# A time-mix layer with a GELU network beside it: k of the first block in halves of 256 tokens, and the third block's loads and statistics behind the first network

## The chip, the core and the metric

The kernel runs on one core of one Trainium2 chip. The metric is the time of one execution on the device in microseconds (us). Nine executions of the kernel before took 942.82 to 943.63 us, with a median of 943.16 us. The engines are called as the profile calls them: PE is TensorE (matmuls; PEld is its weight load), DVE is VectorE, ACT is ScalarE, POOL is GpSimd, and SP is SyncE, which issues nearly all DMAs here.

## The reference

The input x has 4 sequences of 1024 tokens with 512 channels, in float32. Cut to what matters:

```python
xn = (x - mean(x)) / sqrt(var(x) + 1e-5)                       # per token
# attention: a time mix with a decaying state
xx = concatenate([xn[:, 1:2], xn[:, :-1]], axis=1) - xn        # token before; token 1 for token 0
k = einsum('btc,hc->bth', xn + xx * mix_k, Wk)                 # 704 hidden channels
r = einsum('btc,hc->bth', xn + xx * mix_r, Wr)
w = exp(-exp(decay))
state[t] = state[t-1] * w + relu(k[t]);  y[t] = state[t] * r[t]
a = layernorm(einsum('bth,ch->btc', y, Wv)) * gamma + beta
# network on the same xn
d = gelu(float16(xn) @ W0.T + bias0).astype(float16)           # 2048 hidden channels
e = (d @ W1.T + bias1).astype(float16)
out = x + a + e
```

## The kernel before, in words

The tokens go through in 8 blocks of 512. Each block has an attention stage (k, r, the scan over time and the output product) and a network stage, and PE takes them in turn: attention of block 0, then the network of block 0, then attention of block 1, and so on. The 704 hidden channels are five full chunks of 128 (`full_chunks`, lines 391 to 403) and a half chunk of 64 (`half_chunk`, 408 to 421). A chunk's k is four matmuls of 128x512 in float32, one for each 128 channels of x, and so is its r; each float32 matmul shows as two records in the profile. After k, ACT applies the ReLU (line 374), DVE scans (376), and after r DVE multiplies (402). The output product is `attention_out` (425 to 475).

The network (`ffn`, 492 to 545) splits W0 and W1 into a high and a low fp32r part. For each of 16 chunks of its 2048 hidden channels, `up(n)` does eight matmuls into `pd`, ACT applies GELU (510), DVE casts (512), and `down` does eight matmuls into four accumulators `pe` (517). `up` runs two chunks ahead of `down`. In block 0 the network's weights are split while it runs: W0 at line 138, W1 at 153, each by an ACT cast to the high part and a DVE subtraction to the low part (124 and 125); the split W1 is also written to DRAM (154) and read from there by later blocks (156, 147).

For blocks 1 to 7 the inputs are made ahead, inside the network of the block before: `layernorm` (189) with statistics and normalisation on DVE and the inverse root on POOL, `transposed` (198) on DVE, and `mixed_inputs` (334). `load_x` (79) has one buffer, so x of block i+2 can be loaded as soon as block i+1 has been transposed. A scheduler orders the instructions of each engine by its own estimates of their readiness; it may put an instruction earlier than the program text has it.

Block 0 has no block before it, and `first_inputs` (209 to 332) makes its inputs. There the order on ACT, DVE and PE is written out by hand. Four tiles of 128 tokens each are normalised, transposed by PE into four PSUM banks `pts` (one for each 128 channels), and mixed: for each channel chunk and for k and r, ACT scales a copy (313) and DVE adds the token before, scaled (316). PE fills its waiting time with matmuls on the identity (`busy`, 228). Three small transposes belong to it: the mix vectors (282), the first two tokens (278), and the rows of decay and bias0 (295).

PSUM has four banks `ps_mm`, taken in rotation by all products but `pe`, and four banks `ps_e`. The queue of SP is issued in order, and a DMA issue can wait for an earlier DMA to land or for a buffer.

Of the kernel before, what the change touches and what calls it, by code (L numbers as in the profile page):

```python
# [19 lines left out]
def time_mix_and_gelu_ffn(  # L20
# [79 lines left out]
    rest_sb = const.tile([P, 2 * NC], F32, name="rest_sb")  # L100
    w_sb = const.tile([P, NF + 1], F32, name="w_sb")
    b0_sb = const.tile([P, NN], F32, name="b0_sb")
# [7 lines left out]
    nc.sync.dma_start(late_rows[:NF], rows(decay[:H0]))  # L110
    nc.sync.dma_start(late_rows[NF : NF + 1, :HF], decay[H0:].rearrange("(c p) -> c p", p=HF))
    nc.sync.dma_start(late_rows[NF + 1 :], rows(bias0))
    wk_sb = [const.tile([P, HID], F32, name=f"wk_{c}") for c in range(NC)]
    wr_sb = [const.tile([P, HID], F32, name=f"wr_{c}") for c in range(NC)]
    for c in range(NC):
        nc.sync.dma_start(wk_sb[c], wkT[c * P : (c + 1) * P, :])
        nc.sync.dma_start(wr_sb[c], wrT[c * P : (c + 1) * P, :])
    wv_sb = const.tile([P, NF + 1, C], F32, name="wv_sb")
# [21 lines left out]
    def load_w1(i, n):  # L140
        if i == len(blocks) - 1 and n == NN - 1:

            parts = [
                three.tile([P, C], F32R, tag="raw", name=f"w1_{i}_{n}_{p}") for p in range(2)
            ]
            for p in range(2):
                nc.sync.dma_start(parts[p].bitcast(F32), w1_dram[n][:, p, :].bitcast(F32))
            return parts
        w1 = wide.tile([P, 2, C], F32R, tag="w1", name=f"w1_{i}_{n}", bufs=3)
        if i == 0:  # L150
            raw = three.tile([P, C], F32, tag="raw", name=f"w1raw_{n}")
            nc.sync.dma_start(raw, w1T[n * P : (n + 1) * P, :])
            split(w1[:, 0, :], w1[:, 1, :], raw)
            nc.sync.dma_start(w1_dram[n].bitcast(F32), w1.bitcast(F32))
# [43 lines left out]
    def transposed(xn):  # L198
# [3 lines left out]
        for j in range(P // Q):  # L202
            for i in range(P // Q):
# [3 lines left out]
                )  # L207

    def first_inputs(xs, behind):


# [3 lines left out]
        idle = ps_mm.tile([P, TB], F32, tag="mm", name="idle")  # L215
        small = ps_mm.tile([P, TB], F32, tag="mm", name="small")
        tail = ps_mm.tile([P, TB], F32, tag="mm", name="tail")
        mix_t = small[:, : 2 * NC]
        late_t = tail[:, : NF + 1 + NN]
        edge = ps_mm.tile([P, TB], F32, tag="mm", name="edge")  # L220
        edge_t = edge[:, : NC * 2].rearrange("p (c t) -> p c t", t=2)
# [4 lines left out]
        xk = one.tile([P, NC, TB], F32, tag="xk", name="xk_0")  # L226

        def busy(n):
# [15 lines left out]
        def normalized(s):  # L244
            x_s, r = xs[:, s, :], rstd[:, s : s + 1]
            if s < 2:
                shift = shifts[:, s : s + 1]
                nc.vector.scalar_tensor_tensor(
                    shift, mv[:, s, 0:1], -1.0, r, ALU.mult, ALU.mult
                )  # L250
                nc.scalar.activation(x_s, x_s, AF.Identity, bias=shift, scale=r)
            else:
                normalize(x_s, x_s, mv[:, s, 0:1], r)

        def turned(s):
# [7 lines left out]
        steps = [(0, 0), (1, 0), (0, 1), (1, 1), (2, 0), (3, 0), (2, 1), (3, 1)]  # L263
        with tc.manual_schedule(
            engines={nc.scalar.engine, nc.vector.engine, nc.tensor.engine}
        ):

            nc.scalar.activation(shifts[:, :1], eps_sb, AF.Sqrt)
            busy(11)
            stats(0)  # L270
            stats(1)
            deviations(0)
            inverses(0)
            normalized(0)
            normalized(1)
# [6 lines left out]
            nc.tensor.transpose(mix_t, mix_rows, ident[: 2 * NC, : 2 * NC])  # L282
            busy(1)
            stats(2)
            stats(3)
            deviations(2)
            nc.scalar.copy(ends, edge_t)
            nc.scalar.copy(mix_sb, mix_t)
            nc.scalar.activation(rest_sb, mix_t, AF.Identity, bias=1.0, scale=-1.0)
            inverses(2)  # L290
            normalized(2)
            turned(2)
            normalized(3)
            turned(3)
            nc.tensor.transpose(
                late_t, late_rows, ident[: NF + 1 + NN, : NF + 1 + NN]
            )
            busy(5)
# [3 lines left out]
            for dst, m in ((xk[:, :, 0], mk_sb), (xnT[:, :, 1], mr_sb)):  # L302
                part = two.tile([P, NC], F32, tag="part", name="part")
                nc.vector.tensor_mul(part, apart, m)
                nc.vector.tensor_add(dst, part, ends[:, :, 0])
            for c, kind in steps:
                if kind == 0:
                    dst = part = xk[:, c, 1:]
                else:
                    ar = two.tile([P, TB], F32, tag="xx", name=f"ar_0_{c}")  # L310
                    dst, part = xnT[:, c, 2:], ar[:, 1:]
                j = kind * NC + c
                scaled = nc.scalar.activation(
                    part, pts[c][:, 1:], AF.Identity, scale=rest_sb[:, j : j + 1]
                )
                mixed = nc.vector.scalar_tensor_tensor(
                    dst, pts[c][:, : TB - 1], mix_sb[:, j : j + 1], part, ALU.mult, ALU.add
                )

        behind.enter_context(tc.issue_after(scaled.ins))  # L320
        behind.enter_context(tc.issue_after(mixed.ins))
        x16s = []
# [5 lines left out]

        nc.scalar.activation(w_sb, late_t[:, : NF + 1], AF.Exp)
        nc.scalar.activation(w_sb, w_sb, AF.Exp, scale=-1.0)  # L330
        nc.scalar.copy(b0_sb, late_t[:, NF + 1 :])
        return x16s, xk

# [31 lines left out]

    def attention(i, xk):

# [19 lines left out]

        def product(dst, w, cols, src, c):
            nc.tensor.matmul(dst, w[c][:, cols], src, start=(c == 0), stop=(c == NC - 1))  # L389

        def full_chunks():
            g = one.tile([P, NF, TB], F32, tag="g", name=f"g_{i}")
            for h in range(NF):
                cols = slice(h * P, (h + 1) * P)
                pk = ps_mm.tile([P, TB], F32, tag="mm", name=f"pk_{i}_{h}")
                for c in range(NC):
                    product(pk, wk_sb, cols, xk[:, c, :], c)
                st = states(h, P, pk)
                pr = ps_mm.tile([P, TB], F32, tag="mm", name=f"pr_{i}_{h}")
                for c in range(NC):  # L400
                    product(pr, wr_sb, cols, xnT[:, c, 1:], c)
                nc.vector.tensor_mul(g[:, h, :], st, pr)  # L402
            return g
# [79 lines left out]
    def finish(i, s, z, e16):  # L483
        b, t0 = blocks[i]

        width = C // 2 if i == len(blocks) - 1 and s == NS - 1 else C
        for c0 in range(0, C, width):
            cols = slice(c0, c0 + width)
            nc.vector.tensor_add(z[:, cols], z[:, cols], e16[:, cols])
            nc.sync.dma_start(out[b, t0 + s * P : t0 + (s + 1) * P, cols], z[:, cols])  # L490

    def ffn(i, xf, between, state):
# [52 lines left out]
        return pe  # L545

    behind = ExitStack()
    x16s, xk = first_inputs(x_now, behind)
    xf = ffn_input(0, x16s)

    state = {}
    full_chunks, half_chunk = attention(0, xk)
    g = full_chunks()
    gh = half_chunk()
    for i in range(len(blocks)):
# [6 lines left out]
        if more:  # L564
            x_now = load_x(i + 1)

# [3 lines left out]
        def next_norm():  # L570
            layernorm(i + 1, x_now)

# [3 lines left out]

        within = i == 0 or not more
        between = {0: out_stage} if within else {}
        if more:
# [60 lines left out]
```

## Time and profile before

| | us |
|---|---|
| median of nine runs | 943.16 |
| the profiled execution, its own time | 942.84 |
| its span, from the first to the last instruction | 940.9 |
| PE busy in it | 933.9 |
| first k matmul's weight load | 11.14 |
| first matmul of the first network (L502) | 49.34 |
| first k matmul of the second block | 128.86 |
| DVE busy | 486.1 |
| ACT busy | 164.1 |

The profile is of one execution; its clock row grants PE full speed throughout. A timeline row gives the start, the time until the last of its instructions ends, the engine, the line of the code, the operation with output and inputs, how often, and in brackets the idle time before it with what ended that. A row of a table of windows gives, for a stretch of the span, the busy time of each engine. Ends of PE records are modelled and overlap, so the distance from one start to the next is the pace, not the duration of a record.

### The profile page before, as it was taken

What the parts mean: (1) busy time and instruction counts of PE and PEld (TensorE: products, weight loads), DVE (VectorE), ACT (ScalarE), POOL (GpSimd) and SP (SyncE); (2) the same over time, 40 slices, a digit from 0 to 9 for tenths busy, and PEclk for the clock granted to TensorE, in tenths of its full rate; (3) what the DMA queues carried; (4) which work ended last, traced back from release to release, by engine and by line L of the source; (5) the groups of instructions that cost most, each with busy time, mean ns of one, the idle gap of its engine ahead of it and who ended that gap; (6) DMA issues with size and microseconds to landing.
All of it is one profiled execution on the core that took longest, in us unless ns stands there. A gap on an engine that the chain in (4) does not pass through costs nothing.

```text
span 940.9 us, 8730 instructions
## 1 busy us (share of the span) xinstructions
PE 933.9 (99%) x3256; PEld 587.9 (62%) x3256; DVE 486.1 (52%) x843; ACT 164.1 (17%) x266; POOL 52.1 (6%) x124
## 2 busy tenths in 40 slices
PE   9999999999999999999999999999999999999998
PEld 5447754786448864488545885458844588445686
DVE  7568862832927338363483534745356552542513
ACT  6323410220002200022001220012200121001021
POOL 0010000000200001000010000100001000100100
PEclk9999999999999999999999999999999999999999
DMA  9744570343204432044320543105431044210243
GB/s 292 230 148 150 209 246 0 99 170 134 90 0 141 151 112 90 1 157 145 101 90 0 178 136 112 67 0 180 156 112 45 6 151 142 105 45 1 68 156 112
DMA packets 39717, 106.49 MB, mean 113 GB/s; under 512 B 4447, under 2 KB 4732, under 8 KB 39676
## 3 DMA queue, kind: packets, MB, share of 16 engines
q1 hardware_dynamic: 39676, 105.94, 33.4%
q8 instruction: 26, 0.43, 0.2%
q14 instruction: 15, 0.12, 0.0%
HBM read 89.14 MB, written 16.78 MB: 113 GB/s over the span
## 4 chain that ended last, share of the span: by engine, by line
PE 97%; DVE 1%; DMA 1%; ACT 0%; issue 0%; POOL 0%; DVEq 0%; SPq 0%; ACTq 0%
PE pd L502 24%; PE pe L517 24%; PE po L433 15%; PE pr L389 15%; PE pk L389 15%; PE pkr L389 3%; PE po L443 2%; DMA w1raw<-in_L_ffn_W 0%; DMA x<-in_L_attn_x 0%; DVE w L125 0%; PE pt L257 0%; ACT w L124 0%; PE idle L231 0%; DVE stx L183 0%; POOL rx L178 0%
## 5 line engine op out<-in xcount | busy, mean ns | idle before, releaser
L517 PE MATMUL pe<-w,d 128*128 128x512 f32 x1024 | 251.4, 390 | 0.9 <-DVE d L512 0.8
L517 PEld LDWEIGHTS pe<-w,d 128*128 128x128 f32 x1024 | 191.9, 188 | 42.5 <-DVE d L512 2.0
L502 PE MATMUL pd<-xf,w0h 128*128 128x512 f32 x512 | 202.8, 396 | 0.0
L502 PE MATMUL pd<-xf,w0l 128*128 128x512 f32 x512 | 199.3, 389 | 0.0
L510 ACT ACTIVATE d<-pd,b_sb 128x512 f16<-128x512 f32 x128 | 87.9, 687 | 354.1 <-PE pd L502 351.0
L512 DVE CAST d<-d 128x512 fp32r<-128x512 f16 x128 | 54.2, 425 | 183.4 <-ACT d L510 182.1
L389 PE MATMUL pr<-xnT,wr 128*128 128x512 f32 x320 | 144.2, 592 | 0.0
L389 PE MATMUL pk<-xk,wk 128*128 128x512 f32 x320 | 144.1, 592 | 0.0
L433 PE MATMUL po<-wv_sb,g 128*128 128x512 f32 x320 | 140.8, 595 | 0.0
L502 PEld LDWEIGHTS pd<-xf,w0h 128*128 128x128 f32 x512 | 96.1, 188 | 23.3 <-issue 2.3
L502 PEld LDWEIGHTS pd<-xf,w0l 128*128 128x128 f32 x512 | 96.1, 188 | 21.6 <-issue 1.9
L389 PEld LDWEIGHTS pr<-xnT,wr 128*128 128x128 f32 x320 | 60.6, 189 | 76.9 <-issue 74.3
L389 PEld LDWEIGHTS pk<-xk,wk 128*128 128x128 f32 x320 | 60.7, 190 | 75.7 <-issue 73.5
L433 PEld LDWEIGHTS po<-wv_sb,g 128*128 128x128 f32 x320 | 60.1, 190 | 76.0 <-issue 75.1
L204 DVE STREAM_TRANSPOSE xnT<-x 32x512 f32<-32x512 f32 x112 | 78.7, 703 | 5.0 <-PE pkr L389 2.9
L374 ACT ACTIVATE rk<-pk 128x512 f32<-128x512 f32 x40 | 23.9, 597 | 253.1 <-PE pk L389 182.4
L183 DVE BATCH_NORM_STATS2 sty<-po 128x6 f32<-128x512 f32 x32 | 22.1, 691 | 69.2 <-PE po L443 67.0
L376 DVE TENSOR_TENSOR_SCAN st<-w_sb,carry,rk 128x512 f32<-128x512 f32 (+1 forms) x24 | 30.7, 1281 | 48.2 <-ACT rk L374 48.2
L402 DVE TENSOR_TENSOR g<-st,pr 128x512 f32<-128x512 f32 x40 | 27.3, 683 | 46.0 <-PE pr L389 46.0
L376 DVE TENSOR_TENSOR_SCAN st<-w_sb,rk 128x512 f32<-128x512 f32 (+1 forms) x24 | 29.3, 1220 | 33.3 <-ACT rk L374 31.5
L177 POOL TENSOR_SCALAR ry<-mvy 128x1 f32<-128x1 f32 x32 | 11.4, 357 | 439.9 <-DVE mvy L184 439.9
L389 PE MATMUL pkr<-xnT,wr 128*64 128x512 f32 x64 | 29.2, 598 | 0.0
(75 smaller groups left out, 447.7 us busy)
## 6 DMA issues: line engine op xcount, KB each, us to landing
w<-w1d SPq DMA_DIRECT2D x111, 512.0 KB, 3.3
x<-in_L_attn_x SPq DMA_DIRECT2D x32, 256.0 KB, 3.7
xres<-in_L_attn_x SPq DMA_DIRECT2D x32, 256.0 KB, 2.7
w1d<-w SPq DMA_DIRECT2D x16, 512.0 KB, 2.9
out<-z SPq DMA_DIRECT2D x31, 256.0 KB, 2.5
w0raw<-in_L_ffn_W SPq DMA_DIRECT2D x16, 256.0 KB, 4.7
w1raw<-in_L_ffn_W SPq DMA_DIRECT2D x16, 256.0 KB, 3.2
wk<-in_L_attn_Wk SPq DMA_DIRECT2D x4, 352.0 KB, 4.4
```

The lines of the kernel that those rows point to most:

```text
L183: nc.vector.bn_stats(st6, src)
L204: nc.vector.transpose(dst[i * Q : (i + 1) * Q, :, :, j, :], src[j * Q : (j + 1) * Q, :, :, i, :],)
L374: nc.scalar.activation(rk[:hw], pk, AF.Relu)
L376: nc.vector.tensor_tensor_scan(st[:hw], w_sb[:hw, h : h + 1].to_broadcast([hw, TB]), rk[:hw], 0.0 if t0 == 0 else carry[:hw, h : h + 1], A ...
L389: nc.tensor.matmul(dst, w[c][:, cols], src, start=(c == 0), stop=(c == NC - 1))
L402: nc.vector.tensor_mul(g[:, h, :], st, pr)
L433: nc.tensor.matmul(pos[s], g[:, h, s * P : (s + 1) * P], wv_sb[:, h, :], start=(first and h == 0), stop=(not first and h == NF - 1),)
L443: nc.tensor.matmul(pos[s], gh[rows, s // 2, :], wv_sb[rows, NF, :], start=first, stop=not first)
L502: nc.tensor.matmul(pd, w[c][:, cols], xf[:, c, :], start=(c == 0 and w is w0h), stop=(c == NC - 1 and w is w0l),)
L510: state["gelu"] = nc.scalar.activation(d16, pd, AF.Gelu, bias=b0_sb[:, n : n + 1])
L512: nc.vector.tensor_copy(d, d16)
L517: nc.tensor.matmul(pe[s], d[:, s * P : (s + 1) * P], w1[part], start=(n == 0 and part == 0), stop=(n == NN - 1 and part == 1),)
```

## The change

**First block.** The two first token tiles are normalised by two engines: the odd tile by ACT as before, the even tile by DVE. Tiles 2 and 3 are also split in that way. PE turns the mix vectors and the first two tokens ahead of the tiles (both now in one bank, `small`). Then k of three chunks (`pks`) is computed in `first_inputs`, by halves of 256 tokens: `mixed` makes one channel chunk of the first half from the two tiles that are ready, and `products` multiplies it for the three chunks; statistics and normalisation of tiles 2 and 3 stand between these on DVE. PE turns tiles 2 and 3 before the fourth channel chunk of the first half. The second half follows, then r's inputs over all 512 tokens in one piece. `full_chunks` takes these three k as they are and goes on with r. The rows for decay and bias0 are copied from PSUM in one piece (`late_sb`).

**Loads.** The four Wk loads stand ahead of the decay and bias0 rows and of all Wr loads; before, they alternated with Wr.

**Third block.** Its four x loads are issued behind the last W1 write to DRAM (`state["kept"]`). From the second block on, the statistics of the next block stand behind the last addition of the block before (`state["added"]`) on DVE. The half chunk of block 0 stands behind its last r matmul.

The core of the diff:

```diff
     for c in range(NC):
         nc.sync.dma_start(wk_sb[c], wkT[c * P : (c + 1) * P, :])
+    nc.sync.dma_start(late_rows[:NF], rows(decay[:H0]))
...
+    nc.sync.dma_start(late_rows[NF + 1 :], rows(bias0))
+    for c in range(NC):
         nc.sync.dma_start(wr_sb[c], wrT[c * P : (c + 1) * P, :])
...
         def normalized(s):
             x_s, r = xs[:, s, :], rstd[:, s : s + 1]
-            if s < 2:
-                shift = shifts[:, s : s + 1]
+            if s % 2 == 1:
+                shift = shifts[:, s // 2 : s // 2 + 1]
...
+        def mixed(kind, c, a, b):
...
+            j = kind * NC + c
+            one_ = nc.scalar.activation(
+                part, pts[c][:, max(a, 1) : b], AF.Identity, scale=rest_sb[:, j : j + 1]
+            )
+            two_ = nc.vector.scalar_tensor_tensor(
+                dst,
+                pts[c][:, max(a, 1) - 1 : b - 1],
+                mix_sb[:, j : j + 1],
+                part,
...
+        def products(c, part):
+            for h, pk in enumerate(pks):
+                product(pk[:, part], wk_sb, slice(h * P, (h + 1) * P), xk[:, c, part], c)
...
             inverses(0)
+            normalized(1)
             normalized(0)
-            normalized(1)
-            turned(0)
+            nc.tensor.transpose(mix_t, mix_rows, ident[: 2 * NC, : 2 * NC])
             for c in range(NC):
                 nc.tensor.transpose(
                     edge_t[:, c, :], xs[:2, 0, c * P : (c + 1) * P], ident[:2, :2]
                 )
+            turned(0)
             turned(1)
...
+            busy(3)
             nc.scalar.copy(mix_sb, mix_t)
             nc.scalar.activation(rest_sb, mix_t, AF.Identity, bias=1.0, scale=-1.0)
+            nc.scalar.copy(ends, edge_t)
...
+            first_column(xk[:, :, 0], mk_sb)
+            pks = [ps_mm.tile([P, TB], F32, tag="mm", name=f"pk_0_{h}") for h in range(3)]
+            mixed(0, 0, 0, TH)
+            mixed(0, 1, 0, TH)
+            stats(2)
+            mixed(0, 2, 0, TH)
+            stats(3)
+            mixed(0, 3, 0, TH)
+            deviations(2)
+            inverses(2)
+            normalized(3)
+            normalized(2)
+            for c in range(NC):
+                if c == NC - 1:
+                    turned(2)
+                    turned(3)
+                    nc.tensor.transpose(
+                        late_t, late_rows, ident[: NF + 1 + NN, : NF + 1 + NN]
+                    )
+                products(c, halves[0])
+            for c in range(NC):
+                mixed(0, c, TH, TB)
+                products(c, halves[1])
+            first_column(xnT[:, :, 1], mr_sb)
+            nc.scalar.copy(late_sb, late_t)
+            for c in range(NC):
+                scaled, added = mixed(1, c, 0, TB)
...
-                pk = ps_mm.tile([P, TB], F32, tag="mm", name=f"pk_{i}_{h}")
-                for c in range(NC):
-                    product(pk, wk_sb, cols, xk[:, c, :], c)
+                if h < len(pks):
+                    pk = pks[h]
+                else:
+                    pk = ps_mm.tile([P, TB], F32, tag="mm", name=f"pk_{i}_{h}")
...
-    gh = half_chunk()
+    with tc.issue_after(state["pr"].ins):
+        gh = half_chunk()
...
         if more:
-            x_now = load_x(i + 1)
+
+            with tc.issue_after(state["kept"].ins) if i == 1 else nullcontext():
+                x_now = load_x(i + 1)
...
         def next_norm():
-            layernorm(i + 1, x_now)
+            with tc.issue_after(added.ins) if added else nullcontext():
+                layernorm(i + 1, x_now)
```

In the instruction order that the scheduler makes of it, x of block 1 is loaded by four issues in a row ahead of the fourth W0 piece (before, they were spread between W0 pieces), x of block 2 by four issues behind the last W1 write, and block 2's statistics and normalisation stand on DVE between the first scan, the first product and the second scan of block 1's attention. In blocks 3 to 7 the same statistics move by a few places on DVE, behind the additions. The order on POOL is unchanged, and PE's order is unchanged from the fourth chunk of block 0 on.

More of the change, by code (lines that the diff above doesn't have):

```diff
@@ L1 @@
-from contextlib import ExitStack
+from contextlib import ExitStack, nullcontext
 import concourse.bass as bass
@@ L100, in time_mix_and_gelu_ffn @@
     rest_sb = const.tile([P, 2 * NC], F32, name="rest_sb")
-    w_sb = const.tile([P, NF + 1], F32, name="w_sb")
-    b0_sb = const.tile([P, NN], F32, name="b0_sb")
+    late_sb = const.tile([P, NF + 1 + NN], F32, name="late_sb")
+    w_sb, b0_sb = late_sb[:, : NF + 1], late_sb[:, NF + 1 :]
     mk_sb, mr_sb = mix_sb[:, :NC], mix_sb[:, NC:]
@@ L109, in time_mix_and_gelu_ffn @@
     nc.sync.dma_start(mix_rows[NC:], rows(mix_r))
-    nc.sync.dma_start(late_rows[:NF], rows(decay[:H0]))
-    nc.sync.dma_start(late_rows[NF : NF + 1, :HF], decay[H0:].rearrange("(c p) -> c p", p=HF))
-    nc.sync.dma_start(late_rows[NF + 1 :], rows(bias0))
     wk_sb = [const.tile([P, HID], F32, name=f"wk_{c}") for c in range(NC)]
@@ L116, in time_mix_and_gelu_ffn @@
         nc.sync.dma_start(wk_sb[c], wkT[c * P : (c + 1) * P, :])
+    nc.sync.dma_start(late_rows[:NF], rows(decay[:H0]))
+    nc.sync.dma_start(late_rows[NF : NF + 1, :HF], decay[H0:].rearrange("(c p) -> c p", p=HF))
+    nc.sync.dma_start(late_rows[NF + 1 :], rows(bias0))
+    for c in range(NC):
         nc.sync.dma_start(wr_sb[c], wrT[c * P : (c + 1) * P, :])
@@ L153, in load_w1 @@
             split(w1[:, 0, :], w1[:, 1, :], raw)
-            nc.sync.dma_start(w1_dram[n].bitcast(F32), w1.bitcast(F32))
+            kept = nc.sync.dma_start(w1_dram[n].bitcast(F32), w1.bitcast(F32))
+            if n == NN - 1:
+                state["kept"] = kept
         else:
@@ L207, in transposed, with product @@
                 )
+    def product(dst, w, cols, src, c):
+        return nc.tensor.matmul(
+            dst, w[c][:, cols], src, start=(c == 0), stop=(c == NC - 1)
+        )
     def first_inputs(xs, behind):
@@ L216, in first_inputs @@
         small = ps_mm.tile([P, TB], F32, tag="mm", name="small")
+        mix_t = small[:, : 2 * NC]
+        edge_t = small[:, 2 * NC : 4 * NC].rearrange("p (c t) -> p c t", t=2)
         tail = ps_mm.tile([P, TB], F32, tag="mm", name="tail")
-        mix_t = small[:, : 2 * NC]
         late_t = tail[:, : NF + 1 + NN]
-        edge = ps_mm.tile([P, TB], F32, tag="mm", name="edge")
-        edge_t = edge[:, : NC * 2].rearrange("p (c t) -> p c t", t=2)
         mv = two.tile([P, NS, 2], F32, tag="mv", name="mvx_0")
@@ L226, in first_inputs @@
         xk = one.tile([P, NC, TB], F32, tag="xk", name="xk_0")
+        TH = TB // 2
+        halves = slice(0, TH), slice(TH, TB)
         def busy(n):
@@ L259, in turned, with first_column @@
                 )
-        steps = [(0, 0), (1, 0), (0, 1), (1, 1), (2, 0), (3, 0), (2, 1), (3, 1)]
+        def first_column(dst, m):
+            part = two.tile([P, NC], F32, tag="part", name="part")
+            nc.vector.tensor_mul(part, apart, m)
+            nc.vector.tensor_add(dst, part, ends[:, :, 0])
+        def mixed(kind, c, a, b):
+            if kind == 0:
+                dst = part = xk[:, c, max(a, 1) : b]
+            else:
+                ar = two.tile([P, TB], F32, tag="xx", name=f"ar_0_{c}")
+                dst, part = xnT[:, c, 1 + max(a, 1) : 1 + b], ar[:, max(a, 1) : b]
+            j = kind * NC + c
[7 more added lines that the diff above has]
+                part,
+                ALU.mult,
+                ALU.add,
+            )
+            return one_, two_
+        def products(c, part):
+            for h, pk in enumerate(pks):
+                product(pk[:, part], wk_sb, slice(h * P, (h + 1) * P), xk[:, c, part], c)
         with tc.manual_schedule(
@@ L280, in first_inputs @@
                 )
+            turned(0)
             turned(1)
[L282 to L287, printed above, removed]
+            busy(3)
             nc.scalar.copy(mix_sb, mix_t)
             nc.scalar.activation(rest_sb, mix_t, AF.Identity, bias=1.0, scale=-1.0)
-            inverses(2)
-            normalized(2)
-            turned(2)
@@ L293, in first_inputs @@
[L293 to L298, printed above, removed]
+            nc.scalar.copy(ends, edge_t)
             apart = two.tile([P, NC], F32, tag="apart", name="apart")
             nc.vector.tensor_sub(apart, ends[:, :, 1], ends[:, :, 0])
[L302 to L318, printed above, removed]
+            first_column(xk[:, :, 0], mk_sb)
@@ new lines, in first_inputs @@
+            pks = [ps_mm.tile([P, TB], F32, tag="mm", name=f"pk_0_{h}") for h in range(3)]
[15 more added lines that the diff above has]
+                        late_t, late_rows, ident[: NF + 1 + NN, : NF + 1 + NN]
+                    )
+                products(c, halves[0])
@@ L320, in first_inputs @@
+            for c in range(NC):
[5 more added lines that the diff above has]
+                scaled, added = mixed(1, c, 0, TB)
         behind.enter_context(tc.issue_after(scaled.ins))
-        behind.enter_context(tc.issue_after(mixed.ins))
+        behind.enter_context(tc.issue_after(added.ins))
         x16s = []
@@ L327, in first_inputs @@
             nc.scalar.copy(last[:, c, :], pt[:, TB - 1 :])
-        nc.scalar.activation(w_sb, late_t[:, : NF + 1], AF.Exp)
+        nc.scalar.activation(w_sb, w_sb, AF.Exp)
         nc.scalar.activation(w_sb, w_sb, AF.Exp, scale=-1.0)
-        nc.scalar.copy(b0_sb, late_t[:, NF + 1 :])
-        return x16s, xk
+        return x16s, xk, pks
     def mixed_inputs(i, behind):
@@ L364, in ffn_input, with attention @@
         return xf
-    def attention(i, xk):
+    def attention(i, xk, pks=()):
         b, t0 = blocks[i]
@@ L386, in states @@
             return st
-        def product(dst, w, cols, src, c):
-            nc.tensor.matmul(dst, w[c][:, cols], src, start=(c == 0), stop=(c == NC - 1))
         def full_chunks():
@@ L394, in full_chunks @@
                 cols = slice(h * P, (h + 1) * P)
-                pk = ps_mm.tile([P, TB], F32, tag="mm", name=f"pk_{i}_{h}")
-                for c in range(NC):
-                    product(pk, wk_sb, cols, xk[:, c, :], c)
+                if h < len(pks):
+                    pk = pks[h]
+                else:
+                    pk = ps_mm.tile([P, TB], F32, tag="mm", name=f"pk_{i}_{h}")
+                    for c in range(NC):
+                        product(pk, wk_sb, cols, xk[:, c, :], c)
                 st = states(h, P, pk)
@@ L400, in full_chunks @@
                 for c in range(NC):
-                    product(pr, wr_sb, cols, xnT[:, c, 1:], c)
+                    state["pr"] = product(pr, wr_sb, cols, xnT[:, c, 1:], c)
                 nc.vector.tensor_mul(g[:, h, :], st, pr)
@@ L488, in finish @@
             cols = slice(c0, c0 + width)
-            nc.vector.tensor_add(z[:, cols], z[:, cols], e16[:, cols])
+            state["added"] = nc.vector.tensor_add(z[:, cols], z[:, cols], e16[:, cols])
             nc.sync.dma_start(out[b, t0 + s * P : t0 + (s + 1) * P, cols], z[:, cols])
@@ L545, in ffn @@
         return pe
+    state = {}
     behind = ExitStack()
-    x16s, xk = first_inputs(x_now, behind)
+    x16s, xk, pks = first_inputs(x_now, behind)
     xf = ffn_input(0, x16s)
-    state = {}
-    full_chunks, half_chunk = attention(0, xk)
+    full_chunks, half_chunk = attention(0, xk, pks)
     g = full_chunks()
-    gh = half_chunk()
+    with tc.issue_after(state["pr"].ins):
+        gh = half_chunk()
     for i in range(len(blocks)):
@@ L577, in time_mix_and_gelu_ffn @@
         within = i == 0 or not more
+        added = state.get("added")
         between = {0: out_stage} if within else {}
```

## The prediction

> **What bounds the kernel now.** I read the page's busy table first, then a table of windows to find where PE is not at work, then the timeline at those places, and last the waits there.
>
> ```profile
> PE 933.9 (99%) x3256; PEld 587.9 (62%) x3256; DVE 486.1 (52%) x843; ACT 164.1 (17%) x266; POOL 52.1 (6%) x124
> ...
> 0.00:11.14 11.14, 9.42 (x56) 8.51 (x57) 6.43 (x24) 5.21 (x12) 0.69 (x6) 1.00 0.78 238
> ...
> 113.00:174.00 61.00, 60.07 (x189) 33.09 (x188) 31.22 (x51) 8.92 (x15) 1.28 (x2) 1.00 0.30 104
> 174.00:235.00 61.00, 61.00 (x253) 46.56 (x253) 25.15 (x50) 11.01 (x17) 2.08 (x5) 1.00 0.46 155
> ```
>
> The first number after the window is its length, the next is PE's busy time. PE is the bound, and from 11.14 us until its last matmul it is idle only between 113 and 174. So time is to be had in two places: before 11.14, where PE does transposes and fillers but no product, and around 114 and 126. Everything else costs nothing as long as PE stays fed.
>
> ```profile
> 10.34 1.41 DVE L316 SCALAR_TENSOR_TENSOR xk<-pt,mix_sb,xk 128x511 f32<-128x511 f32 x2 [0.38 <-ACT xk L313]
> 11.14 0.30 PEld L389 LDWEIGHTS pk<-xk,wk 128*128 128x128 f32 x2
> ...
> 109.23 1.40 DVE L355 SCALAR_TENSOR_TENSOR xnT<-xx,mix_sb,xnT 128x512 f32<-128x512 f32 x2
> ...
> 114.40 0.43 DVE L512 CAST d<-d 128x512 fp32r<-128x512 f16 x1
> 114.73 1.29 DVE L125 TENSOR_TENSOR w<-w1raw,w 128x512 fp32r<-128x512 f32 x2
> ...
> 112.25 0.39 PE L502 MATMUL pd<-xf,w0h 128*128 128x512 f32 x1
> ...
> 114.88 2.48 PE L517 MATMUL pe<-w,d 128*128 128x512 f32 x8 [0.66 <-DVE d L512]
> 117.20 0.39 PE L502 MATMUL pd<-xf,w0h 128*128 128x512 f32 x1
> ...
> 122.64 4.10 PE L517 MATMUL pe<-w,d 128*128 128x512 f32 x16
> 126.91 2.12 PE L517 MATMUL pe<-w,d 128*128 128x512 f32 x8 [0.17 <-DVE d L512]
> ...
> DVE stx L183 <- DMA x<-in_L_attn_x: 2.0, 2, 1.1
> ```
>
> The first product waits for the mix of the first channel chunk (DVE until 11.08), though all four token tiles had to be turned for it. At 114.88 PE waits for a cast that DVE does late. Undisturbed, a round of eight L502 and eight L517 records takes 3.63 us (108.62 to 112.25). The round from 112.25 takes 4.95, so 1.32 is lost, more than the printed 0.66. Sixteen records from 122.64 should end at 126.27, and the next start at 126.91: 0.64 more. Together 1.96 us.
>
> **The start.** I follow the new order with the old durations. Statistics of tiles 0 and 1, root and inverse are as before. One shift goes (0.06 us of pace), so DVE normalises tile 0 from 5.79 to 6.33 (544 ns, the L187 row) beside ACT's tile 1 from 5.92 to 6.73. Before, ACT did both until 7.44. PE's eleven fillers end at 6.41. The mix transpose comes next; it needs the mix rows. Their queue slots were taken again at 6.37 and 6.84, so they have landed by then: no wait likely, 0.4 us at most. Four edge transposes take 0.34 (7.37 to 7.71), four tile transposes 0.42 each, so the fifth starts at 7.16 and its result is there at 7.45. ACT's three small copies end by 7.1, DVE's three small operations by 7.7.
>
> The half mix isn't in the trace; I interpolate between its own forms. ACT took 0.18 us for 8 columns and 0.68 for 511: 0.44 for 255. DVE 0.17 for 4 and 0.74 for 511: 0.45. So ACT 7.50 to 7.94, DVE to 8.42, first weight load of k at 8.5 in place of 11.14: 2.6 us sooner. The three fillers (0.8 us at the late pace) fit in between.
>
> Then the price. The change makes 24 matmuls of 256 columns from 12 of 512, so 48 records instead of 24. A record of 512 float32 columns is paced at 0.4293 us (3.435 for 8). Half would be 0.215, but each now has its own weight load. The nearest row is the network's: a record with a 188 ns weight load every 0.2266 us. So 48 x 0.2266 = 10.88 against 24 x 0.4293 = 10.30: 0.57 lost (nothing if the pace is 0.215). Between these records lie two tiles' transposes and the tail transpose, which stood ahead of the first product before: 8 x 0.107, 0.13, and 0.17 twice for the change of form, 1.2 us (0.9 without the form change). Three chunks of k end at 8.5 + 10.88 + 1.2 = 20.6; the same work before would end at 11.14 + 0.09 + 10.30 = 21.5. **The start gains 0.9 us** (0 to 1.7).
>
> Does PE get its data? The first-half groups of 1.36 us start at 8.5, 9.86 and 11.22; DVE's second, third and fourth channel chunks, with statistics of tiles 2 and 3 (0.69 each, aggregates 0.1 to 0.2) among them, end at 8.83, 10.02 and 11.21. Root, inverse and shift then take to 11.5; DVE normalises tile 2 to 12.0, ACT tile 3 to 12.4. PE wants them at 12.58 and 13.0, so the cover is half a microsecond. The second half is mixed by 14.3 to 15.5, wanted from 15.15 on in steps of 1.36. Wk goes past Wr and three small rows in SP's queue: issued from 3.3 on, and even the slowest old landing of 5.3 us puts the last by 9.9. It is wanted at 8.5, 9.86, 11.22 and 13.8. Wr is wanted only at 20.6. The decay rows are wanted at 13.6.
>
> A rule of the Trainium skill speaks against the change: TensorE: Matmul & The Clock Gate, section "Why this matters for your kernels", [...] warns that thin matmuls let the clock gate fall back. The row: this trace grants 1.00 throughout, yet the first fillers run at 0.24 us a record and those from 9.94 at 0.13, so there is a cold start that the column doesn't show. It is over by 8.45 (two in 0.28). By the row the 48 records cost 10.9; by the rule, at half clock, 48 x 0.43 = 20.6. I take the row, because the new order has no longer stretch of mere transposes (1.3 us) than the old one, which held its pace after 1.7.
>
> **What is late behind it.** DVE finishes r's inputs at 18.7 (16.0 before), ACT the half-precision copies at 20.3 and after a table load the first ReLU at 22.35 (19.5). PE's second r (24.0) reuses the bank of the first k: cover 1.6 us. The second and third ReLU end at 24.5 and 27.5 behind scans (one `rk` buffer), wanted at 27.4 and 30.9. The W0 splits start about 3 us later, and the four x loads and a residual load of 256 KB now pass the fourth W0 piece: it lands near 28.6 (27.6 before). Products queued behind it on DVE (second at 30.6, third near 33) free banks wanted at 37.7 and 41.2. The loads that stood among later W0 pieces are gone from there, so the stream catches up; the fifth chunk's ReLU and product had 3.4 and 4 us of cover (49.8 for 53.2, 52.6 for 56.7) and now stand earlier in the stream. I count nothing; without that cover, PE would stall by the lateness, 1 to 3 us. Ordering the half chunk and copying decay and bias0 in one piece change nothing on PE.
>
> **Third block.** Away from DVE at 102 to 119: four statistics, four aggregates, four normalisations (5 us), two waits for x (2.0), one for POOL (1.5). Without them DVE goes from its W1 pieces straight to the mix of L355; its eight operations (5.2 us) then start after ACT's half-precision copies, near 104.6, and the late cast comes near 110, right after its GELU (107.7), wanted at 114.07: cover 3.9. The next two W1 splits follow by 111.4. Then the writes, the last W1 loads (issued at 114 in place of 119.94) and their splits run early too; the last one waits for its buffer (119.5), is split by 120.8, and is wanted at 124.9. **1.96 us are gained** (below: 0.6, if the late loads keep part of it). What is late next is nothing near: PE was dense until 112.
>
> Where they land: x is issued after the last W1 write, about 121, ahead of the second network's first W1 loads, which move back by 4 x 0.42 us, to about 126 to 133, and are wanted at 172. On DVE the statistics follow the additions. The chain behind them: the first product moves from 136.6 to about 138, POOL's 1.3 us of inverse root follow, four normalisations of 1.9, and the second scan moves from 140 to about 142. Who waits: PE's third r (146) and fourth r (153), for those products. Covers 8 and 9 us. Block 2's attention already shows this pattern (scan at 259.08 behind a wait on POOL) with PE dense. The moves in blocks 3 to 7 are by under 2 us under the same cover: nothing. The tail is unchanged.
>
> **Sum.** 942.84 - 0.9 - 1.96 = 939.98 for the profiled execution, whose span is 940.9 with 1.9 around it. It lay 0.3 below the median of 943.16, so I predict a median of 940.3.
>
> **Rivals.**
> 1. *The start gives nothing* (15%): Wk, the mix rows or tile 2 come later than reckoned (cover 0.5), so PE waits between the halves what it began sooner. For it: a saturated DMA (share 1.03) in that window. Time 943.16 - 1.96 = 941.2, 941.2 to 941.8.
> 2. *The stalls at 114 and 127 stay in part* (10%): the last W1 pieces were waiting for a DMA (3.4 us in the chain), and three buffers bind it still. Gain 0.9 + 0.6: 941.6.
> 3. *The half products run at half pace* (7%), through the clock or weight loads: 48 records at 0.43, +9.8 on the forecast, 950. Break-even is a pace of 0.2266 + 2.9/48 = 0.287; above 0.327 it is slower by over 0.2%. Against it: the fillers' 0.13 with the same weight load.
> 4. *The first block starves* (6%): products behind W0 pieces come over 4 us late, and PE waits for a bank: 943 to 946.
>
> **Chances.** The forecast has 62%, 939.3 to 941.0: its ends are the start's 0.9 with the pace of 0.215 and no form change, or with half of the gain. Rivals 1 and 2 reach to 942.0. Range 939.3 to 942.0, which leaves out the slower cases and small rests. A measurement here tells 0.2% (1.9 us) from no change: faster by more 0.71, within 0.18, slower 0.11.
>
> **What would show it.** First k weight load near 8.5; 256-column records spaced 0.2266; three k ending near 20.6; no PE idle time from 100 to 130, block 1's first k 2.9 sooner, at 126.0; x of block 2 landed before 131 without a DVE wait. A gap between halves, a spacing over 0.28, or a PE wait between 24 and 60 would make it wrong.

## The result, and the profile after

Nine executions of the changed kernel took 939.44 to 941.13 us, median 939.93; 29 of the kernel before had a median of 943.41. The ratio is 0.9964, with a 95% interval of 0.9956 to 0.9972: 3.5 us faster. The profiled execution took 939.93 with a span of 938.0, against 942.84 and 940.9: 2.9 us. The profiled execution of the kernel before is one of its fastest, and it is the only trace of that kernel.

The busy table and the table of windows of the changed kernel (after the window its length, then the busy times of PE, PEld, DVE, ACT and POOL, PE's granted clock, DMA share and GB/s):

```profile
PE 931.7 (99%) x3274; PEld 591.9 (63%) x3274; DVE 488.4 (52%) x847; ACT 164.7 (18%) x270; POOL 51.4 (5%) x124
...
0.00:9.02 9.02, 7.19 (x42) 6.72 (x42) 3.69 (x15) 3.95 (x10) 0.69 (x6) 1.00 0.76 248
9.02:113.00 103.98, 103.98 (x377) 67.37 (x377) 79.94 (x140) 43.10 (x78) 7.60 (x17) 1.00 0.61 205
113.00:174.00 61.00, 61.00 (x198) 35.07 (x197) 32.78 (x54) 9.47 (x15) 1.27 (x2) 1.00 0.32 114
```

PE's gaps are closed: from 9.02 on its busy time equals the window, and the 0.93 us that were missing between 113 and 174 are there. The timeline at the start:

```profile
6.74 0.20 PE L314 MATMUL small<-ident,mix_rows 8*128 8x8 f32 x1 [0.34 <-DMA mix_rows<-in_L_attn_time_mix_r]
...
8.48 0.87 DVE L288 SCALAR_TENSOR_TENSOR xk<-pt,mix_sb,xk 128x255 f32<-128x255 f32 x2 [0.36 <-ACT xk L285]
9.02 3.75 PEld L213 LDWEIGHTS pk<-xk,wk 128*128 128x128 f32 x18 [0.34 <-DVE xk L288]
9.02 4.15 PE L213 MATMUL pk<-xk,wk 128*128 128x256 f32 x18
...
13.01 1.04 PE L267 MATMUL pt<-ident,x 128*128 128x128 f32 x8
...
14.14 6.74 PE L213 MATMUL pk<-xk,wk 128*128 128x256 f32 x30
...
20.72 3.60 PE L213 MATMUL pr<-xnT,wr 128*128 128x512 f32 x8
```

The first product starts at 9.02 in place of 11.14, though PE had waited 0.34 us for the mix rows. From there to the first r at 20.72 lie the 48 half records and, from 13.01 to 14.14, the transposes of the other two tiles. The end of the first network, with the cast that DVE did too late before:

```profile
108.96 0.42 DVE L546 CAST d<-d 128x512 fp32r<-128x512 f16 x1
...
111.41 0.39 PE L536 MATMUL pd<-xf,w0h 128*128 128x512 f32 x1
...
113.22 1.98 PE L551 MATMUL pe<-w,d 128*128 128x512 f32 x8
115.04 0.39 PE L536 MATMUL pd<-xf,w0h 128*128 128x512 f32 x1
...
120.48 5.61 PE L551 MATMUL pe<-w,d 128*128 128x512 f32 x24
125.92 1.45 PE L213 MATMUL pk<-xk,wk 128*128 128x512 f32 x3
```

The round from 111.41 takes 3.63 us where 4.95 were seen before, and the last 24 records run without a break.

The profile also gives a chain: the work that ended last, followed back step by step to what released it. Its times for PE lie up to 0.2 us behind those of the timeline, so only chains are compared with chains. For the start of the first network and of the second block, the kernel before and then the changed one:

```profile
49.34 3.88 PE pd L502 x16
...
129.03 3.43 PE pk L389 x8
```
```profile
48.52 3.86 PE pd L536 x16
...
126.09 3.43 PE pk L213 x8
```

The first network starts 0.82 sooner and the second block 2.94 sooner. So the first network itself is shorter by 2.12: 77.57 us against 79.69. From there both kernels run at PE's pace; the spans differ by 2.9.

### The profile page after: what moved, and what is told of

Its sections match the earlier page's. It is cut to its first block, busy times and chain, and to the rows that moved or that the text cites. A ratio compares the mean times of both kernels' runs of the same rounds, so it can differ in the third digit from the quotient of the medians.

```text
span 938.0 us, 8777 instructions
## 1 busy us (share of the span) xinstructions
PE 931.7 (99%) x3274; PEld 591.9 (63%) x3274; DVE 488.4 (52%) x847; ACT 164.7 (18%) x270; POOL 51.4 (5%) x124
## 4 chain that ended last, share of the span: by engine, by line
PE 99%; DMA 0%; SPq 0%; DVE 0%; issue 0%; ACT 0%; DVEq 0%; ACTq 0%
PE pd L536 25%; PE pe L551 25%; PE po L467 15%; PE pk L213 15%; PE pr L213 15%; PE pkr L213 3%; PE po L477 2%; DMA mix_rows<-in_L_attn_time_mix_r 0%; SPq L83 0%; PE pt L267 0%; DVE e L514 0%; DVE xk L288 0%; ACT xk L285 0%; DVE z L523 0%; SPq L108 0%
## 5 line engine op out<-in xcount | busy, mean ns | idle before, releaser
L544 ACT ACTIVATE d<-pd,late_sb 128x512 f16<-128x512 f32 x128 | 87.9, 687 | 353.2 <-PE pd L536 353.2
L213 PE MATMUL pk<-xk,wk 128*128 128x512 f32 (+1 forms) x344 | 144.0, 563 | 0.1
L213 PEld LDWEIGHTS pk<-xk,wk 128*128 128x128 f32 x344 | 65.2, 190 | 71.9 <-issue 68.2
L410 DVE TENSOR_TENSOR_SCAN st<-late_sb,carry,rk 128x512 f32<-128x512 f32 (+1 forms) x24 | 30.7, 1280 | 43.9 <-ACT rk L408 43.9
L410 DVE TENSOR_TENSOR_SCAN st<-late_sb,rk 128x512 f32<-128x512 f32 (+1 forms) x24 | 29.2, 1217 | 32.7 <-ACT rk L408 31.0
L514 DVE TENSOR_TENSOR e<-pe,b_sb 128x512 f16<-128x512 f32 x32 | 20.2, 685 | 18.2 <-PE pe L551 18.2
```

The source lines that it names most:

```text
L213: return nc.tensor.matmul(dst, w[c][:, cols], src, start=(c == 0), stop=(c == NC - 1))
L410: nc.vector.tensor_tensor_scan(st[:hw], w_sb[:hw, h : h + 1].to_broadcast([hw, TB]), rk[:hw], 0.0 if t0 == 0 else carry[:hw, h : h + 1], A ...
L514: nc.vector.tensor_add(e16, pe, b1_sb)
L544: state["gelu"] = nc.scalar.activation(d16, pd, AF.Gelu, bias=b0_sb[:, n : n + 1])
```

## The experiments

The theory on record has two parts that add up: the start (0.9 us), and the third block's statistics, for which DVE had waited in order (2 us). Ratios are to runs of the kernel before on the same chip, with 95% intervals.

**The parts, one at a time.** The changed kernel with `with nullcontext():` for both bindings:

> The new start without the two bindings of the third block. Theory (the two parts add up): first k near 9.0 us, first network 0.8 us sooner than before (48.5 in place of 49.3), but the two PE stalls inside the first network remain at some 2 us, so 942.4 to 942.7 against 943.4 before, a ratio of about 0.9991. Rival (the start gives nothing that lasts; the stalls take it back because the late W1 pieces are bound to a DMA and not to PE): stalls grow to 2.9 us, second block's first k at 128.8 as before, ratio 1.000.

The kernel before with the two bindings and nothing else:

> The kernel before with the two bindings alone (third block's x loads behind the last W1 write, statistics behind the last addition). Theory: first k stays at 11.14, no PE idle time from 100 to 130, second block's first k 2.0 to 2.1 us sooner (126.8), 941.3 against 943.4, ratio 0.9978. Rival (the whole gain of 3 us comes from here): ratio 0.9968 or less, first k of the second block near 126.

The start alone: median 942.40 us, ratio 0.9990 (0.9982 to 0.9998). The bindings alone: 940.81, ratio 0.9978 (0.9968 to 0.9988; one of the eight executions took 944.78). In its trace no PE wait stands between these two lines, which come from the timeline and from the chain:

```profile
11.24 0.30 PEld L391 LDWEIGHTS pk<-xk,wk 128*128 128x128 f32 x2
...
127.02 3.43 PE pk L391 x8
```

0.0010 and 0.0022 make 0.0032 of the 0.0036 that both have together; by the medians they gain 1.0 and 2.6 us, against 3.5 together. By this the parts add up as well as the intervals can tell. The single profiled execution of the start alone (942.65) is less clear. By its chain the second block starts at 128.73, only 0.3 us sooner than before the change, though the first network started 0.75 sooner:

```profile
DVE stx L186 <- DMA x<-in_L_attn_x: 2.4, 2, 1.6
...
114.47 2.49 PE L551 MATMUL pe<-w,d 128*128 128x512 f32 x8 [1.01 <-DVE d L546]
...
122.24 6.49 PE L551 MATMUL pe<-w,d 128*128 128x512 f32 x24
```

DVE waits 2.4 us for x of the third block where it waited 2.0 before, and PE's first stall prints 1.01 in place of 0.66. So the rival is partly right in this execution: a PE that arrives sooner waits longer for what a DMA releases.

**Which binding?** Only the loads bound (the second `with` taken out), then only the statistics (the first one taken out):

> The changed kernel with the loads bound but the statistics left to the scheduler, which puts the first of them on DVE ahead of the four additions of bias1, where it has to wait for x. Theory: it waits on DVE up to 1.5 us near 123, at a place where PE doesn't need DVE, so as the changed kernel: 939.9, ratio 0.9964, no PE idle time. Rival (both bindings are needed): a wait of PE near 126 of up to 1.5 us, 941.4.

> The changed kernel with the statistics bound but the loads free, so that the four x loads stand among the last W1 loads on SP again, while DVE's order is exactly the changed kernel's. Theory (the wait of DVE for x did the harm, not the traffic): 939.9, ratio 0.9964, no PE idle time between 100 and 130. Rival (SP's x loads, each waiting for a landing, delay the last W1 pieces): a PE stall of 0.6 us at the last down rounds, 940.5, ratio 0.997.

939.79 and 939.84, ratios 0.9963 (0.9950 to 0.9975) and 0.9964 (0.9951 to 0.9978). Each binding alone does it. With the loads free they are on SP among the W1 loads again, from 97.84 to 103.86, and harm nothing, so the traffic was not the cause:

```profile
97.84 0.80 SPq L83 DMA_DIRECT2D x<-in_L_attn_x  x2
...
102.94 0.92 SPq L83 DMA_DIRECT2D x<-in_L_attn_x  x1
```

With the statistics free, DVE waits longer for x than at any time before the change, at a place where nobody waits for DVE:

```profile
124.98 0.69 DVE L186 BATCH_NORM_STATS2 stx<-x 128x6 f32<-128x512 f32 x1 [2.90 <-DMA x<-in_L_attn_x]
125.59 2.46 DVE L514 TENSOR_TENSOR e<-pe,b_sb 128x512 f16<-128x512 f32 x4
```

PE has no wait there, and the second block starts at 125.72. In the kernel before, the two waits stood ahead of a cast (114.40) and of two W1 splits:

```profile
105.62 0.69 DVE L183 BATCH_NORM_STATS2 stx<-x 128x6 f32<-128x512 f32 x1 [0.87 <-DMA x<-in_L_attn_x]
...
108.62 0.70 DVE L183 BATCH_NORM_STATS2 stx<-x 128x6 f32<-128x512 f32 x1 [1.13 <-DMA x<-in_L_attn_x]
```

So 2.9 us of waiting cost nothing at one place, while a DVE order with 2.0 us of it at another cost PE 2.1. That the waits alone cost this is not shown: with either binding, 5 us of the statistics' and the normalisation's own work and a wait of 1.5 us for POOL left that place too. An estimate from the trace of before: without the 2.0 us the cast would have ended at 112.8, ahead of the 114.07 at which PE wanted it, so the waits would be enough for the first stall.

**Wk ahead of Wr.** The loads' order of before in the changed kernel, the three small rows first:

```diff
+    (decay and bias0 rows)
     for c in range(NC):
         nc.sync.dma_start(wk_sb[c], wkT[c * P : (c + 1) * P, :])
-    (decay and bias0 rows)
-    for c in range(NC):
         nc.sync.dma_start(wr_sb[c], wrT[c * P : (c + 1) * P, :])
```

> The changed kernel with Wk and Wr alternating and the decay and bias0 rows ahead of them, as before the change. Theory (the new start needs Wk sooner than the old order lands it): the second Wk landed near 11.3 before and is now wanted at 10.5, the fourth near 13 and wanted at 14.2, so PE waits up to 1 us in the first halves, 940.4 to 940.9. Rival (Wk's place is without effect): 939.9.

941.77 us, ratio 0.9983 (0.9976 to 0.9990), against 939.48 of the changed kernel on the same chip: 2.3 us, over twice what was expected.

```profile
8.34 1.56 PE L212 MATMUL pk<-xk,wk 128*128 128x256 f32 x6
...
10.07 1.53 PE L212 MATMUL pk<-xk,wk 128*128 128x256 f32 x6 [0.17 <-DMA wk<-in_L_attn_Wk]
...
13.34 1.53 PE L212 MATMUL pk<-xk,wk 128*128 128x256 f32 x6 [1.74 <-DMA wk<-in_L_attn_Wk]
```

The first product is even sooner (8.34), but the third piece of Wk lands only at 13.2. By the chain the first network starts at 50.22 here, against 49.34 in the kernel before: without this order the start's gain of 0.8 would be a loss of 0.9. In this execution PE turns the mix rows at 5.89 without a wait. In those with Wk issued right behind them, they were there at 6.11 to 7.46, or at 6.33 without a wait; one execution is not enough to show that Wk is the reason.

**The mix rows.** They are loaded ahead of the third x tile, with ten fillers in place of eleven:

```diff
         for s in range(NS):
+            if s == 2:
+                amid()          # the two mix_rows loads
             nc.sync.dma_start(xs[:, s, :], x[b, t0 + s * P : t0 + (s + 1) * P, :])
...
-            busy(11)
+            busy(10)
```

> The changed kernel once more, on the same chip as the next three: 939.9, ratio 0.9964.

> The changed kernel with the mix rows loaded ahead of the third x tile and ten fillers in place of eleven. In the changed kernel PE waited for the mix rows until 6.74 us while the first tile was normalised at 6.12. Theory (the mix rows set the start by 0.5 us): the mix transpose near 6.2 or sooner, first k near 8.45 in place of 9.02, and the end 0.5 us sooner, 939.4, ratio 0.9959. Rival (the half mix of the later channel chunks or tile 2 sets it): first k sooner but PE waits between the halves, 939.9.

> The changed kernel with the mix rows early, once more: 939.0 to 939.5, first k near 8.5, and no execution over 941. By the rival that the mix rows are without effect on the time, 939.5 to 939.9, with single executions near 941 as in the changed kernel's first runs (941.13 at most).

The changed kernel again: 939.48 (five runs, 939.39 to 939.65; ratio 0.9960, 0.9948 to 0.9972). With early mix rows: 939.47 (939.40 to 941.06; 0.9964, 0.9951 to 0.9978), and in the second try 939.51 (939.42 to 939.58; 0.9959, 0.9947 to 0.9972). The first k of the changed kernel in that run, and in the two tries:

```profile
8.82 4.15 PE L213 MATMUL pk<-xk,wk 128*128 128x256 f32 x18
```
```profile
8.47 4.15 PE L218 MATMUL pk<-xk,wk 128*128 128x256 f32 x18
```
```profile
8.65 4.15 PE L218 MATMUL pk<-xk,wk 128*128 128x256 f32 x18
```

The spans are 937.8, 937.4 and 937.6. So the traces show 0.2 to 0.35 us in the direction of the theory; the times show no difference. A faster version than the changed kernel is not shown.

**The clock at the start.** All fillers are taken out:

> The changed kernel without the eleven and the three filler matmuls on the identity. Theory (PE starts cold and the halves run at half pace until it is warm): the first halves at 0.43 us a record in place of 0.216 for some 3.4 us or more, so about 8 to 18 of the 48 records cost 0.2 more each, transposes slower as well: 2 to 4 us later, 942 to 944. Rival (the fillers do nothing, as the granted clock of 1.00 would have it): 939.9 or a little less.

942.81 us, ratio 0.9994 (0.9986 to 1.0003): 3.3 us over the changed kernel on the same chip, most of its gain of 3.8 there. The first 18 half records, by the chain, in that run of the changed kernel and without fillers:

```profile
8.82 4.15 PE pk L213 x18
```
```profile
9.41 6.01 PE pk L213 x18
```

They start 0.6 us later and take 6.01 us in place of 4.15. From 9.41 to 13.32 nine of them follow each other at 0.43 us on average, twice the later 0.2156. The clock column grants 1.00 in these windows, so the cold pace is seen only by the distance of the records.

**What a half costs.** k of all other full chunks (37 of them) is done in parts too:

```diff
-                    for c in range(NC):
-                        product(pk, wk_sb, cols, xk[:, c, :], c)
+                    for q in range(2):                     # or 4
+                        part = slice(q * TB // 2, (q + 1) * TB // 2)
+                        for c in range(NC):
+                            product(pk[:, part], wk_sb, cols, xk[:, c, part], c)
```

> The changed kernel with k of the full chunks of all the other blocks, and of block 0's last two chunks, by halves of 256 tokens as well: 37 chunks, 148 matmuls of 512 columns become 296 of 256, so 592 records in place of 296. By the pace of 0.2156 us that the first block's halves show: 592 x 0.2156 = 127.6 against 296 x 0.4293 = 127.1, 0.5 us more than the changed kernel, 940.5. By the forecast's pace of 0.2266 (the network's, with a weight load in each record): 134.1, 7.1 us more, 947.

> As the run with halves, but by quarters of 128 tokens: 1184 records. By columns alone 0.108 a record, 127.9, 0.8 us more than the changed kernel, 940.7. By a weight load that sets the pace (the late fillers of 128 columns ran at 0.12 to 0.13): 1184 x 0.125 = 148, 21 us more, 961. By a weight load that cannot overlap at all (0.19): 225, 98 us more, 1038.

Halves: 940.72, ratio 0.9976 (0.9969 to 0.9983). Quarters: 944.93, ratio 1.0020 (1.0013 to 1.0027). One chunk of k in the second block, by the chain of each (start, length, what, how many records), halves first, then quarters, then the changed kernel:

```profile
128.25 3.45 PE pk L213 x16
```
```profile
127.83 3.57 PE pk L213 x32
```
```profile
126.09 3.43 PE pk L213 x8
```

The lengths give the pace: a half record 0.2156 us, a quarter 0.1116. In halves a chunk costs 0.02 us, 37 of them 0.6; in quarters 0.14, or 5.1. The fastest runs bear this out (940.01 and 944.60 against 939.39 of the changed kernel: 0.6 and 5.2). The weight load prints 190 to 192 ns in all three forms, so it overlaps and doesn't set the pace down to 128 columns.

The starts differ too, and that has another reason. The run with halves had two groups of times: 13 of 18 up to 941.2, five from 942.2 to 942.9. The profiled execution was of the upper one:

```profile
7.60 0.19 PE L314 MATMUL small<-ident,mix_rows 8*128 8x8 f32 x1 [1.51 <-DMA mix_rows<-in_L_attn_time_mix_r]
...
9.00:12.00 3.00, 3.00 (x12) 2.64 (x11) 2.62 (x6) 1.39 (x4) 0.00 (x0) 0.50 0.96 324
```

Here the mix rows came 1 us later than elsewhere, PE had only transposes and a few fillers after 1.5 us of waiting, and the clock column shows half speed just when the half products run: its second block starts at 128.25, over 2 us late. With the mix rows early in that kernel:

> The run with halves in all blocks, with the mix rows loaded early and ten fillers. That run had two groups of times: 13 of 18 from 940.0 to 941.1 and 5 from 942.2 to 942.8, and its profiled execution (942.83) shows the mix rows landing 1 us later than elsewhere (PE waits until 7.60) and a granted clock of 0.50 from 9 to 12 us. Theory (the wait for the mix rows lets the clock fall, and that costs 2 us in some executions): with the rows early no execution is in the upper group, and the clock is 1.00 throughout; all from 939.5 to 941. Rival (the spread is of the chip, or of the halves in later blocks): about a quarter of the executions still near 942.4.

940.50, ratio 0.9971 (0.9962 to 0.9981); seven of ten from 940.1 to 940.7, three from 941.6 to 941.9. The profiled one (940.28) has no such wait and a clock of 1.00. The upper group is closer but not gone, so the wait cannot be all of it.

Two other traces speak against the length of the wait as the cause. In the start alone, PE waited almost as long, and everything behind it ran at the full pace:

```profile
6.82 0.20 PE L314 MATMUL small<-ident,mix_rows 8*128 8x8 f32 x1 [1.40 <-DMA mix_rows<-in_L_attn_time_mix_r]
...
7.18 1.09 PE L267 MATMUL pt<-ident,x 128*128 128x128 f32 x8
...
9.09 4.15 PE L213 MATMUL pk<-xk,wk 128*128 128x256 f32 x18
```

In the profiled execution of the quarters, PE waited a third of that, yet the eight transposes took nearly twice as long, and the first half record began only at 10.49:

```profile
6.86 0.24 PE L314 MATMUL small<-ident,mix_rows 8*128 8x8 f32 x1 [0.45 <-DMA mix_rows<-in_L_attn_time_mix_r]
...
7.45 1.97 PE L267 MATMUL pt<-ident,x 128*128 128x128 f32 x8
...
10.49 3.28 PE L213 MATMUL pk<-xk,wk 128*128 128x256 f32 x14
```

That execution took 946.47, 1.5 us over its median, and the clock column reads 1.00. Its eleven fillers had run for 5.06 us, as in the changed kernel; in the start alone they took 4.07. So the moment at which PE reaches its full pace differs from one execution to the next, and single executions can lose 1.5 us by it. What decides the moment, and what makes three of ten slower with the rows early, stays open.

## Why the prediction was right, point by point

The forecast was 940.3 and a gain of 2.9; the measured median was 939.93. The two profiled executions differ by 2.9, the medians by 3.5. The steps hold for what the traces show; the other 0.6 us is in no step and in no trace, and stays open. By the medians of the parts it lies in both (1.0 where the trace has 0.82, 2.6 where it has 2.12).

- *First k at 8.5*: it was 9.02, so this step was off by 0.5. The wait for the mix rows is 0.34 of it: the forecast allowed for up to 0.4 there, but reckoned with none. The first result of the transposes came 0.1 later than reckoned, and the two mixing steps took a little longer. The rows' landing was taken from the kernel before; in the profiled executions of the new order it varies from 6.11 to 7.46. The first x tile landed 0.2 sooner than before, which no longer mattered.
- *48 half records for 10.88*: from 9.02 to 13.01 and from 14.14 to 20.72 they took 10.57, with some 0.2 of starting up; the pace was 0.2156. I took the network's fp32r row at 0.2266, which has nearly the same weight load (188 ns) but 512 columns of another type; the halves run at half of the float32 record of 512 columns (0.4293). This term was too dear by 0.3.
- *Transposes between them for 1.2*: 1.13. The addends of that term make 1.33, not 1.2. In sum the first r came at 20.7 (forecast 20.6), and the start gained 0.82 in place of 0.9. That is luck in part: a start 0.5 late and two terms too dear nearly cancelled.
- *PE gets its data*: it did, without a wait in the first halves; DVE's tile 2 ended at 12.5 and PE came to it at 12.8, a cover of 0.3 where I had 0.5. The order of the Wk loads was treated as a condition that holds; the run without it shows that it carries more than the start's whole gain.
- *Clock gate, row against rule*: the row was right for this order of work and this execution, and no more than that. Without fillers the first halves run at half the pace, and 3.3 us are gone. This agrees with the Trainium skill (TensorE: Matmul & The Clock Gate, section "Why this matters for your kernels"), which asks for 4 us or more of continuous work to reach the full clock; but in the execution of the quarters 5.06 us of fillers were not enough, and there the measurement decides. The rule on thin matmuls in that section is about steps with a wait for a DMA between them; between these halves PE had none, so the rule did not bear on them.
- *Nothing late behind the start*: right, PE has no wait from 9.02 to 174. The first ReLU ended at 22.4 (forecast 22.35). The second scan of block 1's attention began at 137.5 where 142 was forecast: 2.9 of this is the earlier block, which the 142 did not take off; the rest was not followed up.
- *The stalls at 114 and 127 go, 1.96*: the network is 2.12 shorter. The forecast counted the second loss up to the start at 126.91; the eight records from there to 128.86 took 1.95 where an undisturbed eight take 1.81, and that is the missing 0.14. The late cast ran at 108.96 (forecast near 110), the last W1 loads were issued at 113.4 (114).
- *Rivals*: the start alone is worth 0.0010 and PE has no wait between its halves, so rival 1 falls, though the Wk order shows how near it was. Rival 2 falls with the changed kernel's trace. Rival 3, a half pace over 0.287, falls with 0.2156. Rival 4 is not seen.

What each piece of the new start is worth (the normalising on two engines, the order of the transposes, the halves) was not tried one by one.

## What to carry to other kernels

On an engine that works in order, look at what is queued behind a wait: 2.9 us of waiting at one place of DVE's queue cost PE nothing, while an order with 2.0 us of it ahead of a cast and two splits cost 2.1. Splitting a float32 product to start it early costs little at 256 columns (0.02 us a chunk) and 0.14 us a chunk at 128, but the weights must then be loaded in the order of the new start, or more is lost than gained. The landing of a small load at the head of such a chain is not to be taken from one trace: it varied by over 1 us here. The start of a kernel is best judged by many executions, as PE reaches its full pace at different times.

## What the runs showed of the hardware that was not expected

A 128x128 weight load prints 190 to 192 ns and still lets records of 128 columns follow each other at 0.1116 us. The clock column can grant 1.00 at a pace that is half of the later one (the run without fillers: nine records at 0.43 us on average, 0.2156 later), and shows 0.50 in another execution for the same kind of stretch (9 to 12 us, the run with halves). A wait of 1.51 us stood before that stretch, but behind one of 1.40 the clock stayed at 1.00 and the pace was full; and in the run with quarters PE was still at the slow pace after 5.06 us of fillers and a wait of 0.45.
